# Layer 0's element work laid out anew over ScalarE, VectorE and GpSimd in a two-layer float32 kernel

The kernel runs on one core of a Trainium2 chip. The metric is device time in microseconds (us) of one execution. Every run quoted here was in the undisturbed ("fast") state.

## The reference, cut to what matters

```python
def _block(x, ...):                       # layer 0, on every pixel alone
    t = x.reshape(b, c, h * w).transpose(0, 2, 1)
    t = _ln(t, ln0_g, ln0_b)
    y1 = _ln(t, ln1_g, ln1_b)
    t = t + einsum('btc,oc->bto', sigmoid(y1) * y1, W_out)
    y2 = _ln(t, ln2_g, ln2_b)
    wht = einsum('btc,oc->bto', y2, W_whiten)
    k = square(relu(einsum('btc,hc->bth', wht, W_key)))
    r = sigmoid(einsum('btc,oc->bto', wht, W_recep))
    return t + r * einsum('bth,ch->btc', k, W_value)
# x: [4, 128, 128, 128] float32
x = x + (_block(gn(x)) + the same over the transposed image)
x = x + conv3x3(gn(x)) * se               # layer 1; se = sigmoid of a small net
```

The block treats each pixel by itself, so both passes of layer 0 agree, and the kernel computes one and doubles it.

## The kernel before

An image is cut into 32 chunks of 512 pixels. Every step of the loop issues different stages of four chunks side by side. Each engine works through its own queue in order. That order is the one of the compiled program (the "compiled order"), which is not the order of the source lines: in the traces of the changed kernel, for one, the square of h0, which `keys` issues before `first_norms`, runs behind the normalisation z of `first_norms`. So an edit can also move other instructions in the queues. Layer 0 of image b runs beside the convolution of image b - 1.

```python
def normalize(src, dst):                  # pixels on partitions, four pieces
    for s in range(SUB): nc.vector.bn_stats(...)
    for s in range(SUB): nc.vector.bn_aggr(...)
    nc.vector.tensor_scalar(ve, mv[:, :, 1], LN_EPS, None, ALU.add)
    nc.gpsimd.tensor_tensor(rs, ve, nhalf, ALU.pow)          # 1/std
    for s in range(SUB): nc.vector.tensor_scalar(dst[:, s, :], src[:, s, :], mean, rs, ...)

def first_norms(ut):
    normalize(ut, t)                                         # ln0
    nc.gpsimd.tensor_tensor(t, t, g0, ALU.mult)              # gain
    nc.gpsimd.tensor_tensor(t, t, b0, ALU.add)               # bias
    normalize(t, z)                                          # ln1, goes to silu
...
def silu(z):
    zt = transpose(z, "z1t")
    nc.scalar.activation(sg, flat(zt), AF.Sigmoid, bias=b1, scale=g1)
    nc.vector.tensor_scalar(y, flat(zt), g1, b1, ALU.mult, ALU.add)
    nc.gpsimd.tensor_tensor(y, y, sg, ALU.mult)
...
def turn(z):                                                 # ln2, turned
    nc.scalar.copy(y, flat(transpose(z, "z2t")))

def keys(y):
    for j in range(NH):                                      # four of them
        pk = ps.tile([P, CH], F32, tag="h", name="pk")       # two PSUM buffers
        nc.tensor.matmul(pk, wk_s[:, ts(j, P)], y, start=True, stop=True)
        nc.scalar.activation(h, pk, AF.Relu, bias=kbias[:, j : j + 1])
        nc.scalar.activation(h, h, AF.Square)
    nc.tensor.matmul(pr, wr_s, y, start=True, stop=True)     # pr: tag "h" too
    nc.scalar.activation(r, pr, AF.Sigmoid, bias=rbias)
...
def finish(b, i, r, kv, tt, st1):
    nc.vector.tensor_tensor(r, kv, r, ALU.mult)
    nc.vector.tensor_tensor(r, flat(tt), r, ALU.add)
    nc.vector.scalar_tensor_tensor(xs, r, 2.0, xs, ALU.mult, ALU.add)
    nc.vector.bn_stats(st1[:, i, :], xs)

def layer0(b, mg, rs, st1):
    for n in range(-3, NCH):
        y2 = turn(z2.pop(n))
        y[n + 1] = silu(z1.pop(n + 1))
        hs, r = keys(y2)
        t[n + 2], z1[n + 2] = first_norms(ut.pop(n + 2))
        att = attend(y.pop(n + 1))
        kv, tt = values(hs, t[n])
        z2[n + 1] = second_norm(t[n + 1], att)
        finish(b, n, r, kv, tt, st1)
        ut[n + 3] = lay(b, n + 3, mg, rs)
        yield                              # (conditions at both ends cut)
```

The weight preparation, group norm, the convolution (`conv_chunk`, with its eviction on ScalarE and its residual add on GpSimd) and the outer loop are cut here.

## Time and profile before

| | before |
|---|---|
| time, median of 4 (range) | 3288.28 us (3285.57 to 3290.70) |
| mean granted clock of TensorE | 0.905 |
| mean period of a chunk, layer 0 alone ("alone", 50 periods) | 17.54 us |
| mean period beside the convolution ("mixed", 60 periods) | 24.04 us |

Some 60 chunks run alone and 63 beside the convolution, so 1 us in a period is about 60 us in the whole. Periods are the distances between the evictions of z2t to y, one a chunk. Every fourth mixed chunk also pads an image block for the convolution (a "padding chunk"). How the queues stand inside one chunk is shown in the prediction. The engines are named PE (TensorE), DVE (VectorE), ACT (ScalarE) and POOL (GpSimd), as in the profile; PEld is PE's weight load. "The power" is POOL's 1/std (tile lnrs), "the gain and the bias" are POOL's two operations on t after ln0, and "the gate" is the activation that makes r.

### The profile page before, as it was taken

How to read it: one execution, taken by the hardware profiler on the slowest of the kernel's cores; microseconds unless marked ns; L12 is line 12 of the kernel's file. 1: busy time of each engine (PE TensorE's matmuls, PEld its weight loads, DVE VectorE, ACT ScalarE, POOL GpSimd, SP SyncE). 2: the span in 40 equal slices, each digit the busy share in tenths (PEclk: the TensorE clock that was granted, in tenths of full speed). 3: DMA queues.
4: the chain of work that ended last, by engine and by line, in shares of the span. 5: the costliest groups of instructions: out<-in, count | busy, mean ns of one | idle time of the engine just before them, and what ended most of it. 6: DMA issues, size and time to landing. Idle time of an engine off the chain costs nothing.

```text
span 3285.3 us, 25623 instructions
## 1 busy us (share of the span) xinstructions
PE 2653.4 (81%) x7742; PEld 1331.6 (41%) x7742; DVE 1740.7 (53%) x6162; ACT 956.8 (29%) x1541; POOL 1066.2 (32%) x986
## 2 busy tenths in 40 slices
PE   2777777798888887798888888779788788777999
PEld 1434334344444443344444444334344344343444
DVE  6766766335656556625555655751555545565010
ACT  1334334203233324311333333330222322343101
POOL 2343343133333333314333333321433323332111
PEclk9888888899999898799999988889989989888999
DMA  4000000010000000001000000001000000000000
GB/s 197 1 0 1 0 1 1 7 55 26 23 26 23 26 23 0 1 32 46 26 10 26 23 26 19 1 1 55 16 10 10 13 10 10 7 0 1 32 35 35
DMA packets 25611, 70.21 MB, mean 21 GB/s; under 512 B 3569, under 2 KB 4737, under 8 KB 21377
## 3 DMA queue, kind: packets, MB, share of 16 engines
q1 hardware_dynamic: 23040, 67.12, 5.4%
q10 hardware_dynamic: 2432, 1.46, 0.1%
q8 instruction: 61, 1.00, 0.1%
q14 instruction: 78, 0.63, 0.1%
HBM read 35.02 MB, written 33.55 MB: 21 GB/s over the span
## 4 chain that ended last, share of the span: by engine, by line
DVE 35%; POOL 26%; issue 18%; PE 18%; ACT 1%; DMA 1%; POOLq 0%; SPq 0%; DVEq 0%; ACTq 0%
POOL lnrs L194 11%; DVE z L196 8%; DVE lnst L188 6%; PE pk L267 5%; POOL t L226 5%; POOL t L223 5%; DVE t L196 4%; PE att L246 4%; PE pr L273 3%; DVE lnmv L190 3%; POOL o L364 3%; POOL y L240 3%; DVE r L288 2%; DVE y L239 2%; DVE u L216 2%
## 5 line engine op out<-in xcount | busy, mean ns | idle before, releaser
L358 PE MATMUL pc<-pad,cw 128*128 128x512 f32 x2304 | 1026.9, 599 | 4.2 <-DVE a L326 4.2
L194 POOL TENSOR_TENSOR lnrs<-lnve,nhalf 128x4 f32<-128x4 f32 x384 | 397.6, 1035 | 1140.8 <-DVE lnve L192 1140.0
L358 PEld LDWEIGHTS pc<-pad,cw 128*128 128x128 f32 x2304 | 429.9, 192 | 492.4 <-issue 487.8
L267 PE MATMUL pk<-y,wk_s 128*128 128x512 f32 x1024 | 620.6, 731 | 7.3 <-ACT y L259 7.3
L269 ACT ACTIVATE h<-pk,kbias 128x512 f32<-128x512 f32 x512 | 347.5, 682 | 413.1 <-PE pk L267 412.2
L281 PE MATMUL kv<-h,wv 128*128 128x512 f32 x1024 | 466.3, 598 | 0.0
L196 DVE TENSOR_SCALAR z<-t,lnmv,lnrs 128x128 f32<-128x128 f32 x1024 | 341.8, 396 | 225.9 <-POOL lnrs L194 225.8
L363 ACT ACTIVATE o<-pc,sb,se 128x512 f32<-128x512 f32 x128 | 99.5, 778 | 1158.1 <-issue 639.5
L246 PE MATMUL att<-wo,y 128*128 128x128 f32 x1024 | 195.2, 323 | 273.7 <-POOL y L240 273.7
L188 DVE BATCH_NORM_STATS2 lnst<-t 128x6 f32<-128x128 f32 x1024 | 230.4, 280 | 274.7 <-POOL t L226 272.8
L246 PEld LDWEIGHTS att<-wo,y 128*128 128x128 f32 x1024 | 178.6, 228 | 441.6 <-POOL y L240 344.1
L204 PE MATMUL z2t<-ident,z 128*128 128x128 f32 x512 | 113.0, 343 | 250.5 <-DVE z L196 250.4
L267 PEld LDWEIGHTS pk<-y,wk_s 128*128 128x128 f32 x1024 | 216.1, 237 | 235.6 <-issue 102.8
L270 ACT ACTIVATE h<-h 128x512 f32<-128x512 f32 x512 | 306.2, 623 | 4.2
L364 POOL TENSOR_TENSOR o<-o,x 128x512 f32<-128x512 f32 x128 | 170.0, 1328 | 337.0 <-ACT o L363 337.0
L251 DVE TENSOR_TENSOR t<-att,t 128x512 f32<-128x512 f32 x128 | 88.5, 691 | 360.1 <-PE att L246 359.1
L240 POOL TENSOR_TENSOR y<-y,sg 128x512 f32<-128x512 f32 x128 | 161.9, 1265 | 356.4 <-DVE y L239 354.2
L281 PEld LDWEIGHTS kv<-h,wv 128*128 128x128 f32 x1024 | 190.1, 196 | 187.5 <-issue 154.4
L196 DVE TENSOR_SCALAR t<-ut,lnmv,lnrs 128x128 f32<-128x128 f32 x512 | 175.1, 404 | 133.2 <-POOL lnrs L194 133.2
L348 DVE TENSOR_SCALAR pad<-x,mg,rs 128x128 f32<-128x128 f32 (+1 forms) x88 | 71.7, 850 | 326.5 <-PE pc L358 214.0
L259 ACT COPY y<-z2t 128x512 f32<-128x512 f32 x128 | 74.3, 580 | 519.2 <-PE z2t L204 519.2
L223 POOL TENSOR_TENSOR t<-t,g 128x512 f32<-128x512 f32 x128 | 164.0, 1282 | 184.5 <-DVE t L196 156.3
(65 smaller groups left out, 2166.4 us busy)
## 6 DMA issues: line engine op xcount, KB each, us to landing
x<-in_x SPq DMA_DIRECT2D x32, 1024.0 KB, 4.9
out<-o SPq DMA_DIRECT2D x128, 256.0 KB, 2.0
cw<-in_conv_w ACTq DMA_DIRECT2D x1, 576.0 KB, 8.5
wv<-in_w_value_t ACTq DMA_DIRECT2D x1, 256.0 KB, 5.4
wkt<-in_w_key_t ACTq DMA_DIRECT2D x1, 256.0 KB, 11.6
g<-in_ln_g ACTq DMA_DIRECT2D x1, 64.0 KB, 4.6
b<-in_ln_b ACTq DMA_DIRECT2D x1, 64.0 KB, 4.4
wo<-in_w_out_t ACTq DMA_DIRECT2D x1, 64.0 KB, 2.0
```

The source lines that it names most:

```text
L188: nc.vector.bn_stats(st[:, s, :], src[:, s, :])
L194: nc.gpsimd.tensor_tensor(rs, ve, nhalf, ALU.pow)
L196: nc.vector.tensor_scalar(dst[:, s, :], src[:, s, :], mv[:, s, 0:1], rs[:, s : s + 1], ALU.subtract, ALU.mult,)
L223: nc.gpsimd.tensor_tensor(t, t, g0.rearrange("p (o c) -> p o c", o=1).to_broadcast([P, SUB, C]), ALU.mult)
L240: nc.gpsimd.tensor_tensor(y, y, sg, ALU.mult)
L246: nc.tensor.matmul(att[:, s, :], y[:, ts(s, P)], wo, start=True, stop=True)
L267: nc.tensor.matmul(pk, wk_s[:, ts(j, P)], y, start=True, stop=True)
L269: nc.scalar.activation(h, pk, AF.Relu, bias=kbias[:, j : j + 1])
L270: nc.scalar.activation(h, h, AF.Square)
L281: nc.tensor.matmul(kv, wv[:, j, :], hs[j], start=(j == 0), stop=(j == NH - 1))
L358: nc.tensor.matmul(pc, cw[:, tap, :], pad[:, j * RPC + ky : j * RPC + ky + RPC, kx : kx + W], start=(tap == 0), stop=(tap == 8),)
L364: nc.gpsimd.tensor_tensor(o, o, images[b][k][:, ts(j, CH)], ALU.add)
```

## The change

Its intent is to take work off VectorE and to shorten hand-overs: silu becomes one activation; the sigmoid gates become tanh of the same table, with their affine in existing instructions; ln2's gain and bias move into the eviction that was a bare copy; the four squares and the normalisation of ln0 are dealt out over the engines.

```diff
 def normalize(src, dst, act):
+        if act:
+            nc.vector.scalar_tensor_tensor(nb, mv[:, :, 0], -1.0, rs, ALU.mult, ALU.mult)
         for s in range(SUB):
+            if act:
+                nc.scalar.activation(dst[:, s, :], src[:, s, :], AF.Identity,
+                    bias=nb[:, s : s + 1], scale=rs[:, s : s + 1])
+            else: (as before)
 def first_norms(ut):
-        normalize(ut, t)
+        normalize(ut, t, True)
 def silu(z):
-        nc.scalar.activation(sg, flat(zt), AF.Sigmoid, bias=b1, scale=g1)
-        nc.vector.tensor_scalar(y, flat(zt), g1, b1, ALU.mult, ALU.add)
-        nc.gpsimd.tensor_tensor(y, y, sg, ALU.mult)
+        nc.scalar.activation(y, flat(zt), AF.Silu, bias=b1, scale=g1)
 def turn(z):
-        nc.scalar.copy(y, flat(zt))
+        nc.scalar.activation(y, flat(zt), AF.Identity, bias=b2, scale=g2)
 def keys(y):
-            nc.scalar.activation(h, pk, AF.Relu, bias=kbias[:, j : j + 1])
-            nc.scalar.activation(h, h, AF.Square)
+            nc.scalar.activation(h, pk, AF.Relu)
+            if j == 0:
+                nc.vector.scalar_tensor_tensor(h, pk, 0.0, h, ALU.max, ALU.mult)
+            elif j == 1:
+                nc.gpsimd.tensor_tensor(h, h, h, ALU.mult)
+            else:
+                nc.scalar.activation(h, h, AF.Square)
-        nc.scalar.activation(r, pr, AF.Sigmoid, bias=rbias)
+        nc.scalar.activation(r, pr, AF.Tanh, scale=0.5)
 def finish(b, i, r, kv, tt, st1):
-        nc.vector.tensor_tensor(r, kv, r, ALU.mult)
-        nc.vector.tensor_tensor(r, flat(tt), r, ALU.add)
-        nc.vector.scalar_tensor_tensor(xs, r, 2.0, xs, ALU.mult, ALU.add)
+        nc.vector.scalar_tensor_tensor(r, r, 1.0, kv, ALU.add, ALU.mult)
+        nc.gpsimd.tensor_tensor(r, r, xs, ALU.add)
+        nc.vector.scalar_tensor_tensor(xs, flat(tt), 2.0, r, ALU.mult, ALU.add)
```

Cut: the weight preparation loses the folded gain and biases, the gate of layer 1 becomes a tanh as well, and comments are dropped. The square of h0 on DVE reads the PSUM tile `pk` a second time; before, only the relu on ACT read it.

More of the change, by code (lines that the diff above doesn't have):

```diff
@@ L135, in conv_preact_kernel @@
     wr_s = const.tile([P, P], F32, tag="wr_s", name="wr_s")
-    kbias = const.tile([P, NH], F32, tag="kbias", name="kbias")
-    rbias = const.tile([P, 1], F32, tag="rbias", name="rbias")
     ww = wk.tile([P, P], F32, tag="h", name="ww", bufs=6)
@@ L143, in conv_preact_kernel @@
     nc.scalar.dma_start(wrt, w_recep_t)
-    for src, n, dst, bias in ((wkt, HID, wk_s, kbias), (wrt, P, wr_s, rbias)):
+    for src, n, dst in ((wkt, HID, wk_s), (wrt, P, wr_s)):
         pw = ps.tile([P, CH], F32, tag="h", name="pw")
         nc.tensor.matmul(pw[:, :n], ww, src, start=True, stop=True)
-        raw = wk.tile([P, n], F32, tag="h", name="raw", bufs=6)
-        nc.vector.tensor_copy(raw, pw[:, :n])
-        nc.vector.tensor_scalar(dst, raw, g2, None, ALU.mult)
-        pb = ps.tile([P, CH], F32, tag="h", name="pb")
-        for j in range(n // P):
-            nc.tensor.matmul(pb[:, j : j + 1], raw[:, ts(j, P)], b2, start=True, stop=True)
-        nc.vector.tensor_copy(bias, pb[:, : n // P])
+        nc.vector.tensor_copy(dst, pw[:, :n])
     def group_stats(st, name):
@@ L180, in input_stats, with normalize @@
         return group_stats(st, "0")
-    def normalize(src, dst):
+    def normalize(src, dst, act):
         st = small.tile([P, SUB, 6], F32, tag="lnst", name="lnst")
@@ L194, in normalize @@
         nc.gpsimd.tensor_tensor(rs, ve, nhalf, ALU.pow)
+        if act:
+            nb = small.tile([P, SUB], F32, tag="lnnb", name="lnnb")
+            nc.vector.scalar_tensor_tensor(nb, mv[:, :, 0], -1.0, rs, ALU.mult, ALU.mult)
         for s in range(SUB):
-            nc.vector.tensor_scalar(
-                dst[:, s, :], src[:, s, :], mv[:, s, 0:1], rs[:, s : s + 1],
-                ALU.subtract, ALU.mult,
-            )
+            if act:
+                nc.scalar.activation(
+                    dst[:, s, :], src[:, s, :], AF.Identity,
+                    bias=nb[:, s : s + 1], scale=rs[:, s : s + 1],
+                )
+            else:
+                nc.vector.tensor_scalar(
+                    dst[:, s, :], src[:, s, :], mv[:, s, 0:1], rs[:, s : s + 1],
+                    ALU.subtract, ALU.mult,
+                )
     def transpose(src, name):
@@ L229, in first_norms @@
         z = wk.tile([P, SUB, C], F32, tag="z1", name="z1")
-        normalize(t, z)
+        normalize(t, z, False)
         return t, z
@@ L235, in silu @@
         zt = transpose(z, "z1t")
-        sg = wk.tile([P, CH], F32, tag="sg", name="sg")
-        nc.scalar.activation(sg, flat(zt), AF.Sigmoid, bias=b1, scale=g1)
         y = wk.tile([P, CH], F32, tag="y", name="y")
-        nc.vector.tensor_scalar(y, flat(zt), g1, b1, ALU.mult, ALU.add)
-        nc.gpsimd.tensor_tensor(y, y, sg, ALU.mult)
+        nc.scalar.activation(y, flat(zt), AF.Silu, bias=b1, scale=g1)
         return y
@@ L252, in second_norm @@
         z = wk.tile([P, SUB, C], F32, tag="z2", name="z2")
-        normalize(t, z)
+        normalize(t, z, False)
         return z
@@ L268, in keys @@
             h = wk.tile([P, CH], F32, tag="h", name="h", bufs=6)
-            nc.scalar.activation(h, pk, AF.Relu, bias=kbias[:, j : j + 1])
-            nc.scalar.activation(h, h, AF.Square)
+            nc.scalar.activation(h, pk, AF.Relu)
[3 more added lines that the diff above has]
+                nc.gpsimd.tensor_tensor(h, h, h, ALU.mult)
+            else:
+                nc.scalar.activation(h, h, AF.Square)
             hs.append(h)
@@ L329, in squeeze @@
         se = stat.tile([P, 1], F32, tag="se", name="se")
-        nc.scalar.activation(se, p2[:, 0:1], AF.Sigmoid)
+        nc.scalar.activation(se, p2[:, 0:1], AF.Tanh, scale=0.5)
+        nc.vector.tensor_scalar(se, se, 0.5, 0.5, ALU.mult, ALU.add)
         sb = stat.tile([P, 1], F32, tag="sb", name="sb")
```

## The prediction

> **What bounds the kernel now.** I read the page first, then the busy time by stretches, then the timeline and the chain of waits inside one chunk of each stage.
>
> ```profile
> PE 2653.4 (81%) x7742; PEld 1331.6 (41%) x7742; DVE 1740.7 (53%) x6162; ACT 956.8 (29%) x1541; POOL 1066.2 (32%) x986
> ...
> 200.00:400.00 200.00, 150.27 (x484) 81.65 (x483) 136.95 (x522) 77.82 (x128) 78.79 (x69) 0.85 0.00 1
> ...
> 800.00:1000.00 200.00, 170.77 (x517) 84.91 (x515) 116.37 (x412) 62.82 (x102) 70.39 (x64) 0.94 0.06 22
> ```
>
> No engine is full. Two stages make most of the time. From 74 to 613 us, and at the end of each later image, layer 0 runs alone ("alone"). Between, each chunk of layer 0 runs beside one chunk of the convolution ("mixed"). The copy of line 259 runs once a chunk, so its distance is the period. Alone:
>
> ```profile
> 1302.48 0.59 ACT L259 COPY y<-z2t 128x512 f32<-128x512 f32 x1 [9.49 <-PE z2t L204]
> ...
> 1303.54 4.79 PE L267 MATMUL pk<-y,wk_s 128*128 128x512 f32 x6
> ...
> 1307.25 1.01 POOL L194 TENSOR_TENSOR lnrs<-lnve,nhalf 128x4 f32<-128x4 f32 x1 [0.44 <-DVE lnve L192]
> ...
> 1308.29 1.37 DVE L196 TENSOR_SCALAR t<-ut,lnmv,lnrs 128x128 f32<-128x128 f32 x4 [1.12 <-POOL lnrs L194]
> ...
> 1309.80 1.28 POOL L223 TENSOR_TENSOR t<-t,g 128x512 f32<-128x512 f32 x1 [1.54 <-DVE t L196]
> ...
> 1311.17 1.27 POOL L226 TENSOR_TENSOR t<-t,b 128x512 f32<-128x512 f32 x1
> ...
> 1318.37 1.12 DVE L196 TENSOR_SCALAR z<-t,lnmv,lnrs 128x128 f32<-128x128 f32 x4 [0.93 <-POOL lnrs L194]
> ...
> 1320.05 0.58 ACT L259 COPY y<-z2t 128x512 f32<-128x512 f32 x1 [8.29 <-PE z2t L204]
> ```
>
> The period is 17.57 us, with DVE busy 12. The bound is latency: DVE goes in order through three layer norms, each with a trip to POOL for its power (1.0 us), and the first waits for the gain and the bias on POOL (2.6 us). ACT is far from it. Mixed:
>
> ```profile
> 903.09 0.58 ACT L259 COPY y<-z2t 128x512 f32<-128x512 f32 x1
> ...
> 903.89 2.93 PE L267 MATMUL pk<-y,wk_s 128*128 128x512 f32 x6
> ...
> 907.17 1.27 POOL L364 TENSOR_TENSOR o<-o,x 128x512 f32<-128x512 f32 x1
> 907.23 2.06 DVE L196 TENSOR_SCALAR z<-t,lnmv,lnrs 128x128 f32<-128x128 f32 x4 [1.13 <-POOL lnrs L194]
> ...
> 909.21 0.80 DVE L239 TENSOR_SCALAR y<-z1t,g,b 128x512 f32<-128x512 f32 x1
> ...
> 910.09 1.26 POOL L240 TENSOR_TENSOR y<-y,sg 128x512 f32<-128x512 f32 x1 [1.65 <-DVE y L239]
> ...
> 911.40 0.96 PE L246 MATMUL att<-wo,y 128*128 128x128 f32 x4 [4.58 <-POOL y L240]
> ...
> 927.90 0.58 ACT L259 COPY y<-z2t 128x512 f32<-128x512 f32 x1
> ```
>
> Here the period is 24.8 us; over the chunks from 740 to 1214 us it is 20.5 to 26.2, mean 23.7. PE waits 4.6 us for silu, because line 239 stands behind the normalisation z in DVE's queue although its sigmoid was ready at 904.3; then PE runs slow for a while. The waits add up in the list of waits:
>
> ```profile
> PEld att L246 <- POOL y L240: 344.1, 101, 7.2
> PE att L246 <- POOL y L240: 273.7, 71, 6.4
> ```
>
> **What the Trainium skill says.** (1) "TensorE: Matmul & The Clock Gate", Part 1: after an idle window of about 3.4 us the array runs at half clock until it has been busy for such a window. The trace agrees: six key matmuls take 4.79 us alone, behind an idle PE, and 2.93 us mixed, behind a busy one; the waits of 4.6 us cost some 2 us more. (2) "GPSIMD Engine Reference", section 4.1: two-input elementwise work is about twice as slow there as on VectorE. The trace: 1.27 us against 0.69 us. (3) The same page, section 1: its SBUF interface is shared with VectorE's two-port modes. The trace: z takes 2.06 us beside line 364 and 1.12 us without. (4) "ScalarE: Activation LUTs", What ACT_TABLE_LOAD costs: every function has one rate, a per-partition pointer costs about 93 ns, a table load 1283 ns. The trace: 784 ns with scale and bias pointers, 682 with bias, one load of 1283 ns. The compiled order of the changed kernel has two loads in all, both before the first chunks, so silu and tanh do share a set.
>
> **The change part by part, per chunk.**
> - Silu: removed are DVE 0.80, POOL 1.27 and two hand-overs; one activation of 0.78 us gives y. PE's wait at att goes. Good for up to 4.6 + 2 us in the mixed stage, taken alone.
> - First normalisation to ACT: DVE loses 1.37 us and gains 0.16 (the bias). ACT gains four 128x128 activations with two pointers: 784 ns less 384 x 0.833 is 464 ns for one, about 0.37 each in a row, so 1.6 us. This lies on the chain and is 0.4 us longer than before with its extra hop.
> - Squares: ACT loses two of 0.62; DVE gains one scalar_tensor_tensor (0.68), POOL one of 1.27.
> - Finish: DVE loses one of 0.69, POOL gains one of 1.27, with a new dependence DVE, POOL, DVE.
> - Affine on the eviction: the copy goes from 0.58 to 0.78 us.
> Sums: DVE 12.1 to about 10.1, ACT about 0.5 more, POOL 6.9 to 8.2. None comes near the period. So what counts is where the new pieces stand in the in-order queues, and I read that from the compiled order of the changed kernel.
>
> *Alone.* It repeats in a cycle of four chunks. I set the durations above along that order, with 0 at the end of the second normalisation; as in the trace before, the first relu runs at 3.6 and the second ends at 5.9 (PE is cold).
> - Kind 1: POOL squares h1 (5.95 to 7.25) before the gain; t is ready at 9.9 (before: 10.5), the rest adds 7.6: 17.6.
> - Kind 2: POOL has the h1 square before the power of the first norm. DVE is ready for this at 5.35, POOL begins it at 7.3, ACT gets the bias at 8.5. And ACT's four pieces of t stand between relu, square and gate, the last behind the gate: t is done at about 13, gain and bias at 15.8. The residual add then stands before the power of the second norm (1.3). Sum 24.2.
> - Kind 3: t goes ahead of the relus, the square between gain and bias: 16.8.
> - Kind 4: t's last piece behind the third relu (8.5), gain and bias to 11.2, the residual add before the last power: 19.7.
> The mean is 19.6 us against 17.6; I take 19.4. Some 60 periods are of this kind: 60 x 1.8 = +110 us.
>
> *Mixed.* Att no longer waits, but the third key matmul now needs the PSUM buffer that DVE frees with its square of h0 (line 269), and in all steady mixed chunks this stands behind z, where line 239 stood before z in half of them. From the end of PE's ut transposes: first power at 4.0, bias 5.2, t on ACT to 6.9, gain and bias to 9.6, statistics and power to 12.1, z to 13.2 or, beside the residual add of the convolution, 14.2, the square to 13.9 or 14.9. PE arrives at 10.9 and so waits 3.0 to 4.0 us; after it come two keys, gate, kv and transposes, 7.1 us, and up to 2 us for the cold clock. The period is 21 to 24, in chunks that also pad 25, before 20.5 to 26.2. I take 23.7 as before: 63 periods, 0 us.
>
> Start, ends and the 8 convolution chunks between images (8 us each, PE-bound) hardly change. Sum: 3288 + 110 + 0 = about 3400 us.
>
> **Rivals.**
> (a) The silu wait was the cost and nothing takes its place. Then mixed chunks fall to PE's work of about 18.5 us plus 1 (63 x 4.2 = 265 us), and alone the 2 us off DVE come back (60 x 1.5 = 90): about 2930 us. For it: the 344 us of waits. Against it: the square of h0 behind z.
> (b) Mixed as I have it but with waits of 3 us too short for the cold clock, period 21.5 (-140 us), and alone the mean is only 18.2 (+40): about 3190 us.
> (c) The delays compound: POOL's and ACT's queues block each other in mixed chunks too, as in kind 2: mixed 25, alone 20: +230, about 3520 us.
>
> **Range and chances.** My own reading gives 3400. The least certain terms are kind 2 (one quarter of 60 chunks, 5 us at stake, so 75 us) and the cold clock in mixed chunks (2 us x 63, so 125 us). So 3220 to 3540 should hold it 8 times in 10. Faster by over 2% (below 3222) needs (a) or a strong (b): 0.12. Slower by over 2% (above 3354): 0.62. Within: 0.26.
>
> **What would show it right or wrong.** Right: alone, the second-norm activations (once a chunk) come at uneven distances in a cycle of four, one over 22 us and one under 17.5; there, the power of line 185 waits behind the square of line 271, and pieces of t on ACT stand between relus. Mixed: no wait of att on silu; in its place PE waits for DVE h of line 269, some 3 to 4 us a chunk, and mean clock is no higher than 0.905. POOL is busy about 170 us more, DVE about 250 less. Wrong: if the list of waits shows no DVE h ahead of pk, or periods alone are even and under 17.5, then (a) holds and the queues did not bind as I set them out; if mixed periods are near 21 with a warm clock, (b).

## The result, and the profile after

| | before | after |
|---|---|---|
| time, median of 4 (range) | 3288.28 us (3285.57 to 3290.70) | 3428.35 us (3425.83 to 3432.96) |
| ratio, with 95% interval | | 1.0424 (1.0409 to 1.0440) |
| mean granted clock | 0.905 | 0.890 |
| alone / mixed mean period | 17.54 / 24.04 us | 18.68 / 25.48 us |

The change made the kernel 4.2% slower. A ratio is the mean time of one kernel's fast runs over that of the other's in the same rounds, so it is not quite the ratio of the medians quoted.

From the page of the changed kernel, the engines' busy time and the groups of the key matmul and of the normalisation z (busy us, mean ns of one, then idle time just before them and what ended it):

```profile
PE 2698.2 (79%) x7732; PEld 1337.1 (39%) x7732; DVE 1503.9 (44%) x5650; ACT 983.3 (29%) x1798; POOL 1190.7 (35%) x1114
...
L265 PE MATMUL pk<-y,wk_s 128*128 128x512 f32 x1024 | 677.3, 797 | 318.1 <-DVE h L269 296.8
...
L196 DVE TENSOR_SCALAR z<-t,lnmv,lnrs 128x128 f32<-128x128 f32 x1024 | 386.2, 439 | 265.0 <-POOL lnrs L185 265.0
```

DVE does 237 us less than before and POOL 124 more, and yet the kernel is slower. PE now stands idle for 297 us just before the key matmul (last column), where before it was 7. The instruction that it waits for is DVE's square of h0, line 269. The list of waits of the changed kernel (total, times, longest) says the same, and shows a second wait that has grown from 273 us: DVE's statistics waiting for the bias of ln0 on POOL.

```profile
PE pk L265 <- DVE h L269: 296.8, 73, 6.0
...
DVE lnst L179 <- POOL t L226: 484.1, 127, 6.8
```

The windows of the changed kernel, with the busy time of PE, PEld, DVE, ACT and POOL, then clock, DMA share and GB/s, answer to the two of before:

```profile
200.00:400.00 200.00, 141.00 (x443) 76.52 (x442) 103.19 (x458) 70.64 (x136) 83.92 (x75) 0.81 0.00 0
800.00:1000.00 200.00, 163.51 (x477) 79.85 (x476) 97.04 (x345) 61.00 (x111) 73.90 (x68) 0.90 0.06 21
```

In both stages the clock fell (0.85 to 0.81, 0.94 to 0.90) and PE was busy less. Now the timeline of one mixed chunk of the changed kernel (start, duration; in brackets the idle time just before, and what ended it):

```profile
919.09 0.60 ACT L267 ACTIVATE h<-pk 128x512 f32<-128x512 f32 x1 [0.55 <-PE pk L265]
...
921.67 1.26 POOL L368 TENSOR_TENSOR o<-o,x 128x512 f32<-128x512 f32 x1
921.74 2.78 DVE L196 TENSOR_SCALAR z<-t,lnmv,lnrs 128x128 f32<-128x128 f32 x4 [1.12 <-POOL lnrs L185]
922.89 1.04 POOL L271 TENSOR_TENSOR h<-h 128x512 f32<-128x512 f32 x1
924.45 0.68 DVE L269 SCALAR_TENSOR_TENSOR h<-pk,h 128x512 f32<-128x512 f32 x1
...
925.18 3.38 PE L265 MATMUL pk<-y,wk_s 128*128 128x512 f32 x4 [4.60 <-DVE h L269]
```

The relu of h0 is done at 919.69. Its square could run then, but it stands behind z in DVE's queue, and so it runs at 924.45. Only then is the first `pk` buffer free, and PE, which has waited 4.60 us, gets its third key matmul. z itself takes 2.78 us, because two POOL operations, the residual add and the square of h1, run beside it one after the other. Asked for piece by piece, with narrow windows, the trace shows the first three of z's four pieces:

```profile
921.74 1.28 DVE L196 TENSOR_SCALAR z<-t,lnmv,lnrs 128x128 f32<-128x128 f32 x1 [1.12 <-POOL lnrs L185]
...
922.93 1.07 DVE L196 TENSOR_SCALAR z<-t,lnmv,lnrs 128x128 f32<-128x128 f32 x1
...
923.93 0.33 DVE L196 TENSOR_SCALAR z<-t,lnmv,lnrs 128x128 f32<-128x128 f32 x1
```

The first ends 0.08 us after the residual add, the second 0.08 us after the square of h1; the last two take 0.33 us each. So z is not slowed evenly: one piece of it lasts until the POOL operation beside it is over.

The timeline of one chunk alone of the changed kernel, from one eviction of z2t to the next, 23.3 us later:

```profile
340.07 0.78 ACT L256 ACTIVATE y<-z2t,b,g 128x512 f32<-128x512 f32 x1 [7.68 <-PE z2t L204]
...
345.67 1.04 POOL L271 TENSOR_TENSOR h<-h 128x512 f32<-128x512 f32 x1 [4.08 <-ACT h L267]
346.67 1.01 POOL L185 TENSOR_TENSOR lnrs<-lnve,nhalf 128x4 f32<-128x4 f32 x1
...
351.42 0.49 ACT L191 ACTIVATE t<-ut,lnnb,lnrs 128x128 f32<-128x128 f32 x1
351.99 1.27 POOL L223 TENSOR_TENSOR t<-t,g 128x512 f32<-128x512 f32 x1 [4.31 <-ACT t L191]
...
354.64 0.87 DVE L179 BATCH_NORM_STATS2 lnst<-t 128x6 f32<-128x128 f32 x4 [6.76 <-POOL t L226]
...
363.36 0.78 ACT L256 ACTIVATE y<-z2t,b,g 128x512 f32<-128x512 f32 x1 [11.44 <-PE z2t L204]
```

The power of ln0 at 346.67 comes after the square of h1, which has waited for a relu. The four pieces of t on ACT, begun at 347.91, end at 351.91, because relus, squares and the gate stand between them. DVE then idles for 6.76 us.

**Where the 139 us went.** The profiled spans differ by 138.8 us. The 60 mixed periods add 87, the 50 alone ones 57, the three steps from image to image 5, the end 2; the start gives back 9 and the 14 other periods 3. The sum is 139 us.

### The profile page after: what moved, and what is told of

Same layout as the page of the kernel before. It is cut to its first block, busy times and chain, and to the rows that moved or that the text cites. A ratio compares the mean times of both kernels' runs of the same rounds, so it can differ in the third digit from the quotient of the medians.

```text
span 3424.1 us, 25272 instructions
## 1 busy us (share of the span) xinstructions
PE 2698.2 (79%) x7732; PEld 1337.1 (39%) x7732; DVE 1503.9 (44%) x5650; ACT 983.3 (29%) x1798; POOL 1190.7 (35%) x1114
## 5 line engine op out<-in xcount | busy, mean ns | idle before, releaser
L265 PE MATMUL pk<-y,wk_s 128*128 128x512 f32 x1024 | 677.3, 797 | 318.1 <-DVE h L269 296.8
L196 DVE TENSOR_SCALAR z<-t,lnmv,lnrs 128x128 f32<-128x128 f32 x1024 | 386.2, 439 | 265.0 <-POOL lnrs L185 265.0
L267 ACT ACTIVATE h<-pk 128x512 f32<-128x512 f32 x512 | 305.6, 597 | 597.2 <-PE pk L265 595.3
L265 PEld LDWEIGHTS pk<-y,wk_s 128*128 128x128 f32 x1024 | 231.0, 250 | 573.0 <-DVE h L269 313.6
L191 ACT ACTIVATE t<-ut,lnnb,lnrs 128x128 f32<-128x128 f32 x512 | 202.1, 460 | 752.2 <-DVE lnnb L188 752.2
L291 POOL TENSOR_TENSOR r<-r,x 128x512 f32<-128x512 f32 x128 | 162.2, 1267 | 256.1 <-DVE r L290 192.3
L256 ACT ACTIVATE y<-z2t,b,g 128x512 f32<-128x512 f32 x128 | 100.7, 787 | 512.2 <-PE z2t L204 512.2
L204 PEld LDWEIGHTS z2t<-ident,z 128*128 128x128 f32 x512 | 73.3, 151 | 332.2 <-issue 295.0
L271 POOL TENSOR_TENSOR h<-h 128x512 f32<-128x512 f32 x128 | 133.5, 1043 | 125.3 <-ACT h L267 111.7
```

The lines of the kernel that those rows point to most:

```text
L191: nc.scalar.activation(dst[:, s, :], src[:, s, :], AF.Identity, bias=nb[:, s : s + 1], scale=rs[:, s : s + 1],)
L196: nc.vector.tensor_scalar(dst[:, s, :], src[:, s, :], mv[:, s, 0:1], rs[:, s : s + 1], ALU.subtract, ALU.mult,)
L204: nc.tensor.transpose(pt[:, s, :], src[:, s, :], ident)
L267: nc.scalar.activation(h, pk, AF.Relu)
L291: nc.gpsimd.tensor_tensor(r, r, xs, ALU.add)
```

## The experiments

Ratios are to the kernel before of the same rounds (median of before 3287 to 3290 us). All results were correct.

| run | what is different | median us | ratio (95%) | alone / mixed us |
|---|---|---|---|---|
| changed | | 3428.35 | 1.0424 (1.0409 to 1.0440) | 18.68 / 25.48 |
| e1_sbuf_square | changed; square of h0 reads SBUF | 3162.16 | 0.9616 (0.9600 to 0.9632) | 19.14 / 20.97 |
| e2_last_key | changed; DVE squares h3, not h0 | 3241.98 | 0.9861 (0.9846 to 0.9875) | 20.41 / 20.87 |
| e3_squares_act | changed; squares back on ACT | 3184.73 | 0.9688 (0.9674 to 0.9702) | 20.38 / 20.03 |
| e4_silu_alone | before; silu and gates only | 2858.34 | 0.8692 (0.8679 to 0.8705) | 16.12 / 18.75 |
| e5_norm_dve | changed; ln0 back on DVE | 3402.62 | 1.0342 (1.0326 to 1.0357) | 18.63 / 25.38 |
| e6_gpsimd_square_act | changed; square of h1 back on ACT | 3350.93 | 1.0181 (1.0164 to 1.0197) | 18.37 / 24.45 |
| e7_norm_and_squares_back | e3 and e5 together | 2925.17 | 0.8892 (0.8878 to 0.8907) | 16.54 / 19.36 |
| e8_and_finish_back | e7, and the add of finish back on DVE | 2865.99 | 0.8712 (0.8699 to 0.8725) | 16.28 / 18.82 |
| e9_silu_deeper | e4, with one more chunk in flight | 2763.14 | 0.8402 (0.8388 to 0.8416) | 14.29 / 18.77 |
| e10_changed_deeper | changed, with one more chunk in flight | 3041.14 | 0.9238 (0.9218 to 0.9257) | 16.74 / 20.91 |

The theory: silu as one activation is a large gain, and the places of the other moved pieces in the in-order queues cost more than it. In the mixed stage that is the `pk` buffer held until DVE's square; alone it is POOL's square before the power, and t's pieces among ACT's other work. The rival: the new split simply has more or slower work (slower z, more POOL time), wherever it stands.

### Who holds the PSUM buffer

```diff
 e1_sbuf_square:
-                nc.vector.scalar_tensor_tensor(h, pk, 0.0, h, ALU.max, ALU.mult)
+                nc.vector.tensor_tensor(h, h, h, ALU.mult)
 e2_last_key:
-            if j == 0:
+            if j == NH - 1:
```

> The same as the changed kernel, but VectorE squares the first key's h from SBUF (h*h) and not from PSUM: same engine, same count, and in the mixed stage the same place in VectorE's queue, behind z. Only the PSUM buffer is freed by ScalarE's relu. Buffer theory (the third key matmul waits for that buffer): the wait of the key matmul on VectorE's h, 297 us, vanishes; a shorter one of about 2.4 us a chunk stands before the first value matmul; mixed period from 25.5 to 20.5-21.5 (63 x -4.3 = -270 us). Alone, the compiled order has ScalarE's pieces of t between relus in every chunk: period 19 to 20 against a mean of 18.8 (+70 us). Sum about 3220 us. Load theory (VectorE and GpSimd are slowed by the added element work and their shared port, the buffer is incidental): 3380 to 3440 us.

> The changed kernel with VectorE's square on the fourth key instead of the first, still from PSUM. Buffer theory: the third key's buffer is freed by ScalarE; the fourth key's buffer is needed only by the next chunk's first key, so the wait moves behind three value matmuls and nearly goes: mixed 20 to 21 (-300 us). Alone, ScalarE's last piece of t stands behind the gate in every chunk: about 20.5 (+100 us). Sum about 3230 us. Load theory: no change, 3400 to 3450.

Both keep the number of squares on each engine; e1 does the same multiplication at the same place of the program, on DVE, but no longer reads `pk`. In all 60 mixed chunks the order of the instructions on DVE, ACT and POOL is the same in both traces, and z is as slow as before (440 ns for a piece on average, 439 in the changed kernel). The mixed period fell from 25.48 to 20.97 us, and the whole by 8%. This settles the larger part of the mixed stage, 4.5 of the 6.7 us between the changed kernel and e4: that cost was the second reader of the buffer, not the amount of work. Alone the compiled order is another one, and the period rose to 19.14 us, as expected. In the list of waits of e1, no wait of pk on DVE's square is left. A smaller one has moved to the value matmul, which needs the squared h itself:

```profile
PE kv L284 <- DVE h L269: 88.3, 51, 2.9
```

e2 gives the same mixed period (20.87), since the buffer of the last key is next taken by the first key of the next chunk, most of a period later. Alone it is slower than the changed kernel, 20.41 against 18.68. DVE waits some 5 us a chunk there for the relu of h3, with the square of h3 in its queue (295 us in the list of waits of e2, 70 times), but this wait is not what makes the chunk long. In e3, below, DVE has no square at all, and its chunk alone is as long (20.38); in both, the gain on POOL starts 9.1 us after the eviction of z2t, released by t on ACT. Here are these gains, of e2 and of e3:

```profile
314.45 1.27 POOL L223 TENSOR_TENSOR t<-t,g 128x512 f32<-128x512 f32 x1 [2.69 <-ACT t L191]
...
316.21 1.27 POOL L223 TENSOR_TENSOR t<-t,g 128x512 f32<-128x512 f32 x1 [6.40 <-ACT t L191]
```

What the two share is that t's last piece stands behind the gate on ACT in every chunk, as the expectations have it; in the changed kernel it does so in one chunk of four. So position matters in both stages: that of DVE's square in the mixed one, and alone, in these two runs, that of t's pieces on ACT.

### All squares back on ACT

```diff
-            if j == 0: (DVE) / elif j == 1: (GpSimd) / else:
-                nc.scalar.activation(h, h, AF.Square)
+            nc.scalar.activation(h, h, AF.Square)
```

> The changed kernel with all four squares on ScalarE, as before the change. Buffer theory: no wait on VectorE's h in PE's list; mixed about 19.5, near PE's own work (63 x -6 = -380 us). Alone: two pieces of t stand behind the gate on ScalarE in every chunk, so that the gain starts at about 10 us and the period is 20 to 21 (60 x +2 = +120 us), if t in ScalarE's queue is what costs there; if the squares' load on VectorE and GpSimd cost, alone falls to 17.5 or below. Sum about 3170 us, or under 2980.

Mixed chunks came to 18.8 us, but most padding chunks of two images to 24 to 27 (of the last image to 20); the mean is 20.03. Alone the period is even, 20.4 us, although neither DVE nor POOL has a square any more. What is left of the change there is above all ln0's normalisation on ACT, among four relus and now four squares. The expectation did not have the long chunks. The list of waits of e3 shows where PE waits:

```profile
PEld pk L265 <- ACT y L256: 120.7, 72, 5.7
```

The key matmuls wait for the eviction of z2t, which stands in ACT's queue behind t's four pieces; in a padding chunk DVE is late with what these need, so that they begin some 12 us after the ut transposes instead of 6. A queue that was hardly loaded (ACT is busy 34% of e3's span) still passes one engine's lateness on to PE.

### Silu alone

```diff
 before, silu():
-        nc.scalar.activation(sg, flat(zt), AF.Sigmoid, bias=b1, scale=g1)
-        nc.vector.tensor_scalar(y, flat(zt), g1, b1, ALU.mult, ALU.add)
-        nc.gpsimd.tensor_tensor(y, y, sg, ALU.mult)
+        nc.scalar.activation(y, flat(zt), AF.Silu, bias=b1, scale=g1)
 keys(), with rbias halved when it is made:
-        nc.scalar.activation(r, pr, AF.Sigmoid, bias=rbias)
+        nc.scalar.activation(r, pr, AF.Tanh, bias=rbias, scale=0.5)
 finish(), all on VectorE:
+        nc.vector.scalar_tensor_tensor(r, r, 1.0, kv, ALU.add, ALU.mult)
+        nc.vector.scalar_tensor_tensor(r, flat(tt), 2.0, r, ALU.mult, ALU.add)
+        nc.vector.tensor_tensor(xs, r, xs, ALU.add)
 (the gate of layer 1 as in the change)
```

> The kernel before with only silu as one activation (and gates as tanh, so that one table serves; the finish keeps three VectorE operations, squares stay on ScalarE, normalisation on VectorE, biases folded). Theory that the silu wait was the cost and the rest of the change gave it back: no wait of att on GpSimd; mixed from 23.7 to about 19.5 (63 x -4.2 = -265 us), alone from 17.6 to about 16.2 (60 x -1.4 = -85 us): about 2940 us. Rival (the silu wait is hidden behind another, VectorE's chain is as long without it): mixed above 22, over 3150 us.

Silu alone here means silu with the gates, which share its table. It is 13% faster than before: the gain was there all along. The window of 800 to 1000 us of e4 reads:

```profile
800.00:1000.00 200.00, 197.53 (x651) 99.94 (x650) 127.75 (x486) 79.83 (x132) 76.56 (x73) 1.00 0.08 29
```

PE is busy 99% of the time at full clock, with most mixed chunks at 18.3 us. Without the wait PE does not cool down either, so two gains come together; that this is the reason why it beats the sum expected is likely, but no run takes the two apart.

### Undoing the other parts, one and two at a time

```diff
 e5_norm_dve, first_norms():
-        normalize(ut, t, True)
+        normalize(ut, t, False)
 e6_gpsimd_square_act, keys():
-            elif j == 1:
-                nc.gpsimd.tensor_tensor(h, h, h, ALU.mult)
 e7_norm_and_squares_back: both edits of e3 and e5
```

> The changed kernel with the first normalisation back on VectorE; squares on three engines and the rest as changed. Theory: VectorE's square still stands behind z and holds the third key's buffer in the mixed stage, so mixed stays at about 24.8; alone, no pieces of t in ScalarE's queue, but in every second chunk GpSimd still has the h1 square before the power: two kinds of about 17.2 and 19.5, mean 18.2. Sum about 3428 - 45 - 30 = 3350 us. If ScalarE's pieces of t were all that cost alone, 16.5 there and 3240 in sum.

> The changed kernel with the GpSimd square of the second key back on ScalarE; VectorE's square from PSUM stays. Theory: mixed keeps its wait on VectorE's h, but z runs beside one GpSimd operation and not two (2.05 us in place of 2.79): 24.8. Alone, kind 2 (23.3 us) is gone, since nothing stands before the power; ScalarE's pieces of t between relus remain in every chunk: all near 19. Sum about 3428 - 45 + 20 = 3400 us. If load on GpSimd were the cause, alone under 17.5 and 3310 in sum.

> The changed kernel with two parts undone: all squares on ScalarE and the first normalisation on VectorE; silu, tanh, affine on the eviction and the finish with an add on GpSimd stay. Theory: both queue effects are gone. Mixed 18.3 to 20, mean 19.2; alone, the gain starts at about 5.4 us after the second normalisation and the chain is some 15 us. Sum about 3428 - 400 - 220 = 2810 us. If the GpSimd add of the finish costs alone as in the changed kernel's kinds 2 and 4 (1.3 us before a power), 2870 us.

Taking ln0 off ACT by itself gave only 26 us, and the period alone did not move (18.63 us). The two kinds of chunk that were expected came, at 17.8 and 19.8 us, but each longer than set, and the mixed period was 25.38 us and not 24.8; the sum missed by 53 us. The timeline of the longer kind, every second chunk alone, shows what holds ln0:

```profile
368.56 0.69 DVE L269 SCALAR_TENSOR_TENSOR h<-pk,h 128x512 f32<-128x512 f32 x1 [1.44 <-ACT h L267]
369.17 0.16 DVE L183 TENSOR_SCALAR lnve<-lnmv 128x4 f32<-128x4 f32 x1
369.86 1.04 POOL L271 TENSOR_TENSOR h<-h 128x512 f32<-128x512 f32 x1 [6.29 <-ACT h L267]
...
370.86 1.01 POOL L185 TENSOR_TENSOR lnrs<-lnve,nhalf 128x4 f32<-128x4 f32 x1
```

DVE waits 1.44 us for a relu, with the variance of ln0 (line 183) next in its queue; then the power of ln0 waits behind POOL's square, which waited 6.29 us for another relu. In this kind the norm is tied to the relus through the squares, although DVE finishes it. e6 missed in the other direction: it was expected at 3400 us and came at 3350.93. It made the alone periods nearly even (17.7, 18.9, 18.0) and took about 1 us off the mixed ones, where all but the squares keep their order and z beside one POOL operation takes 2.05 us again.

Together the two undoings are worth far more than their sum. By the medians, e5 takes 26 us off the changed kernel, e3 takes 244, and e7 takes 503. The periods show that this happens alone: 18.68 us in the changed kernel, 18.63 without the first detour, 20.38 without the second, 16.54 without both. (In the mixed stage the parts nearly add: 0.1 and 5.5 us against 6.1.) Either detour by itself leaves the chain of ln0 behind the keys in some or all chunks. But alone, each undoing also brought another compiled order, so these numbers price an edit together with the order that came with it; no run takes the two apart. e7 came 55 to 115 us above the two sums expected.

### The add of finish

```diff
 e8_and_finish_back:
-        nc.gpsimd.tensor_tensor(r, r, xs, ALU.add)
+        nc.vector.tensor_tensor(r, r, xs, ALU.add)
```

> As the last, with the finish's add on VectorE as well: of the change only silu, tanh and the affine on the eviction stay. The same bounds as the run with silu alone (2858 us), less the bias pointers of relu (0.09 us each) and the hand-over: mixed 18.5, alone 15.7, sum about 2830 us. If above 2880, the eviction's second pointer costs.

It takes 59 us off e7 and, at 2866 us, stays 36 above the sum expected. The timeline of e7, alone, shows what the add on POOL did there:

```profile
345.38 1.26 POOL L286 TENSOR_TENSOR r<-r,x 128x512 f32<-128x512 f32 x1
345.45 2.04 DVE L196 TENSOR_SCALAR z<-t,lnmv,lnrs 128x128 f32<-128x128 f32 x4 [0.52 <-POOL lnrs L185]
```

z takes 2.04 us beside it and 1.12 without, so an add of 0.69 us saved on DVE came back as 0.92 us on the piece that starts the next transposes. This is the smaller part. By the periods of the profiled runs the 59 us are 32 mixed, 13 alone and 13 elsewhere, and most of the mixed part lies in three padding chunks each of two images (21 to 23 us in e7, 18.4 in e8); how the add does it there was not traced. What still separates e8 from e4 (affine on the eviction, no biases on the relus) is worth 8 us.

So the 140 us (by the medians, 3428.35 - 3288.28) come apart along one path of kernels. Silu and gates give 430 us (before to e4); the affine, with the relus' biases gone, costs 8 (e4 to e8), finish 59 (e8 to e7), and squares and ln0 together 503 (e7 to changed): -430 + 8 + 59 + 503 = 140.

### Is a chunk alone bound by latency or by work?

```diff
 e9 (from e4) and e10 (from the changed kernel): first_norms() ends after the
 bias of ln0, the normalisation of ln1 is called one step later; t in 5 buffers
-        for n in range(-3, NCH):
+        for n in range(-4, NCH):
...
-                t[n + 2], z1[n + 2] = first_norms(ut.pop(n + 2))
+                z1[n + 2] = second_of_first(t[n + 2])
+            if 0 <= n + 3 < NCH:
+                t[n + 3] = first_norms(ut.pop(n + 3))
...
-            if n + 3 < NCH:
-                ut[n + 3] = lay(b, n + 3, mg, rs)
+            if n + 4 < NCH:
+                ut[n + 4] = lay(b, n + 4, mg, rs)
```

> The run with silu alone, with the first norm's two halves issued for different chunks (the normalisation with gain and bias one chunk ahead of the second normalisation, one more t buffer): no element work is added or taken. If alone is bound by the latency of one chunk's chain (VectorE, GpSimd and back, 2.6 us for gain and bias), alone falls from 16.1 to about 13.5 and PE idles less and is warm; mixed stays at 18.5. Sum 2858 - 60 x 2.6 = about 2700 us. If VectorE's work bounds it, no change: 2830 to 2870.

> The changed kernel, all its parts kept, with the same deeper order. VectorE's square of the first key still stands behind z in the queue, but z no longer waits for this chunk's gain and bias, so that the square comes early. If queue positions and not the amount of work made the changed kernel slow, mixed falls from 25.5 to about 19.5 and alone from 18.7 to about 15: 3428 - 63 x 6 - 60 x 3.7 = about 2830 us. If the split of work itself is slow (port sharing, hand-overs), above 3200.

With the same instructions as e4, e9 brought the period alone from 16.12 to 14.29 us. If the amount of work had been the bound, it would have stayed. The hoped-for sum of 2700 us was missed by 63 us: alone the period fell by 1.83 us and not by 2.6 (some 46 us over 60 chunks), and the step from one image to the next went up from 124 to 131 or 132 us (23 us for the three). The mixed stage kept its mean (18.77 us against 18.75), since padding chunks of two images went up to between 22 and 26 us while others came down to 18.3. e9 is the fastest of all, 16% under the kernel before.

e10 was a test of the whole explanation: if places in the queues were everything, the changed split should come near e9 once its chain has slack. It gained 11% on the changed kernel but stayed 278 us above e9, between the two sums expected (2830, or above 3200): alone 16.74 us and mixed 20.91, where about 15 and 19.5 were expected. So a place one chunk later heals a good part, not all. In its list of waits the same queues still hold PE and DVE up:

```profile
DVE h L272 <- ACT h L270: 268.4, 106, 5.7
...
PE pk L268 <- ACT y L259: 138.9, 69, 5.2
PE z1t L204 <- DVE x L295: 134.8, 50, 4.3
```

DVE waits for a relu before it may square, and PE waits for an eviction on ACT and for finish on DVE. How much of the 278 us is z made slower by POOL's extra work, and how much is these waits, no run separates.

## Why the prediction was right, point by point

The time (3428 us against 3400) and the class were right, and the two mechanisms on which it stood were seen in the trace. The one of the mixed stage is confirmed by e1, the one alone by e7 as a whole, without a share for each of its parts. The two sizes in the sum were off in opposite directions, so the total is nearer than its terms, which is luck.

- **Silu's wait goes, another takes its place.** Right. Att waits on silu only 6 times, 11 us in all. The square of h0 stands behind z in each of the ten mixed chunks from 807 to 1062 us; PE waits 3.7 to 6.0 us there, where 3.0 to 4.0 was predicted. e1 shows that the buffer is the cause.
- **Mixed stage, 0 us.** Wrong in size: the periods measured say 1.44 x 63, about +90 us. By the prediction's clock (0 at the end of the ut transposes, 909.20 in the chunk shown) the first power came at 4.6 (4.0 predicted), t was done at 7.3 (6.9), gain and bias at 10.0 (9.6), the power at 12.5 (12.1). z ended at 15.3 instead of 13.2 or 14.2, and the square at 15.9 instead of 13.9 or 14.9. Some 0.4 to 0.6 us is a first power mis-set, and the rest is the mis-sized term: z beside one POOL operation was set at 2.06 us, but the change puts h1's square right behind the residual add, and z took 2.78. e6, without that square on POOL, has z at 2.05 us and a mixed period 1.03 us shorter. What follows PE's wait took 8.8 to 10.1 us in these chunks; 7.1 plus up to 2 was predicted.
- **Padding chunks, 25 us.** Nine of fifteen took 26.8 to 27.6, with the square's wait at 6.0 us in the two looked at.
- **Alone, a cycle of four.** Right in shape, somewhat high in size: 16.3, 23.3, 15.7 and 19.8 us were measured for 17.6, 24.2, 16.8 and 19.7. Over 60 periods that is about +70 us and not +110. Of the queue positions named, both were seen in the long chunk: the power behind POOL's square, and the last piece of t behind the gate. Two terms of the sum are measured: the h1 square was set at 1.27 us and takes 1.04, and ACT's piece of t was set at 464 ns, 1.6 us for four, and takes 460, with 1.50 for four in a row.
- **Signs.** DVE -237 us (about -250 predicted), POOL +124 (about +170; 128 squares that are 0.23 us cheaper are 29 of the difference), clock 0.890 (no higher than 0.905).
- **Rival (a), silu's wait was the cost and nothing replaces it.** Its first half is true and was priced too low: e4 is worth 430 us, where the rival had 355. Its second half is what fails in the changed kernel. **Rival (b)** expected short waits with a warm clock; they were not. **Rival (c)**, queues that block each other in mixed chunks too, at 25 us there, described the mixed stage better than my own reading did, and its value alone (20 us) was too high.
- **What the prediction did not see.** It priced each part by itself along one order. It did not foresee that ln0's move and the squares lock each other, so that undoing them is not additive (26, 244 and 503 us). Nor did it see that padding chunks would stay long when the square was out of the way: with t's pieces ahead of ACT's evictions in e3, and without them, somewhat less, in e7.

## What to carry to other kernels

When work moves between engines, busy time says little: ask for every moved instruction which buffer it frees, and what stands ahead of it in its in-order queue. An instruction that reads PSUM a second time on a busy queue can hold the matmuls back, and reading the SBUF copy in its place cost nothing here and gave 8%. Test a bundle of edits part by part and in pairs, since here one of its parts (silu with its gates) was worth 13% and with a deeper order 16%, while the bundle lost 4%.

## What the Trainium skill lacked or had wrong

- "GPSIMD Engine Reference", section 1 (Specifications), names the contention with VectorE's two-port modes without a size; other pages of the skill say more of its form. Here four 128x128 float32 tensor_scalar took 1.12 us by themselves, 2.04 to 2.07 beside one 128x512 GpSimd operation of 1.26 us, and 2.78 beside two in a row. Beside one operation, one of the four lasted until that operation was over (1.28 us, ending 0.08 us after it), and the other three took 0.33 each.
- The same page, section 3.1, has one rate for two-input elementwise work. Here a 128x512 float32 multiplication of a tile by itself (h by h) took 1.04 us, and one of two different tiles 1.27.
- "ScalarE: Activation LUTs", the list of table sets, has no row that names silu. In this kernel silu, tanh, relu, square and identity run through all 128 chunks on two table loads of 1283 ns, the second of them just before the first silu.
- No page that I read says that a second reader of a PSUM tile on another engine's in-order queue can hold matmuls back: 297 us of PE's idle time in the changed kernel, none of it in e1.
